# A decoder layer on one core: all transposes on TensorE, v truncated by three engines, and a new order

## The chip, the cores and the metric

The kernel runs on one NeuronCore of a Trainium2 chip. That core has TensorE (PE, matrix products into PSUM), VectorE (DVE), ScalarE (ACT), GpSimd (POOL) and SyncE (SP, which issues the DMAs here). The metric is the device time in microseconds, as the median of several runs. A profile is one further execution, recorded instruction by instruction. Its span runs from the first to the last instruction.

## The reference

One decoder layer, in pre-norm form, on x of 16 x 128 x 256 in float32 with a context of 16 x 128 x 128:

```
x = x + attn(layernorm(x))             # A: fixed-point self attention, 16 heads of 64
x = x + xattn(layernorm(x), ctx)       # B: cross attention to ctx, 16 heads of 64
x = x + ffn(layernorm(x))              # C: two LoRA experts on one shared FFN, 256 -> 1024 -> 256
```

Attention A rounds nearly everything toward zero to a grid of 1/4096:

```
make_fxp(x) = trunc(clip(x, -c, c) * 4096) / 4096
q, k, v = make_fxp(split(x @ w_qkv.T))
dots = make_fxp((q @ k.T) / 8);  attn = make_fxp(softmax(dots))
out = make_fxp(attn @ v);        out = make_fxp(out @ w_proj.T + b_proj)
```

B is a plain softmax attention with an output projection. C adds `top_k_values[k] * relu(x @ (wi + lora_k).T) @ wo.T` over two experts.

## The kernel before

The 16 sequences are worked on as 8 blocks of two (BLK = 2, so 256 tokens, blk 0 to 7). A and B split the 16 heads into two halves of 8 (hf). For each block the program lists its operations in this way: prep A, attn_A for both halves, out_proj A, prep B, ctx_prep, attn_B for both halves, out_proj B, prep C, ffn.

Each operation is recorded first (`Recorder.op`) with its engine, an estimated cost, and the tiles it reads and writes. A list written out by hand, `ORDER` (lines 39 to 119), then gives the order in which the 2,019 recorded operations are emitted. Each engine runs its own operations strictly in that order, and SP issues its DMAs in that order as well. So a wait at the head of one engine's queue holds up everything that stands behind it on that engine. The estimated costs served to make the list; they have no effect on the chip. Several blocks are under way at once: while one block is in attention A, others are in B or C.

Tiles are given slots. In SBUF there are the classes L, M, S and T. In PSUM there are three "big" slots of 4,096 bytes per partition and two "sml" slots of 2,048 bytes. A tile that finds no free slot waits until the last reader of the former owner is done.

To keep float32 accuracy with float16 matrix products, a value is split into hi (float16) and lo (the rest, float16), and a product takes three passes: hi*hi, hi*lo, lo*hi (`PASSES`). So most matmuls are float16 ones of 128x256 (lines 489, 607, 761, 799) or 128x512 (line 499). Scores (line 540) and the product with v of B (line 679) are smaller and run two at a time on halves of the array. The product with v of A (line 583) is float32, and each of those matmuls is two passes in the records.

The parts that the change touches:

- `prep` (lines 424 to 462) normalizes x to xh (float32, tokens on partitions) and needs it transposed as hi and lo, xTh and xTl. For three preps (A of blocks 0 and 1, C of block 7; `BY_PE`) PE transposes xh into a sml PSUM tile pt, ACT copies the hi part out (line 451) and DVE subtracts for the lo part (line 452). For the other 21, ACT makes hi (line 455), DVE makes lo (line 456), and SP issues a DMA transpose of each (lines 457 and 458).
- `attn_A` makes q, k and v as integers on the grid. ACT computes a positive and a negative part in two passes, p and n (lines 507 and 508), and DVE subtracts them; for v that is line 553. After softmax, POOL multiplies by the reciprocal sums and rounds down to int16, one instruction for each of 8 heads (a_A, line 571). SP transposes the tile by DMA (line 574), POOL casts it to float32 (aTf_A, line 576), and PE multiplies with v (line 583).
- `attn_B` has POOL multiply the exponentials by the reciprocal sums (line 660), POOL make the hi part ah (line 661) and DVE the lo part al (line 662). SP transposes both by DMA (line 669), and PE multiplies with v (line 679).
- Another helper, `trunc1` (line 510), truncates in one pass of ACT (line 513) and one of DVE (line 514). Before, it serves only the output of A's attention.

Of the kernel before, what the change touches and what calls it, by code (L numbers as in the profile page):

```python
# [8 lines left out]
F32 = mybir.dt.float32  # L9
F16 = mybir.dt.float16  # L10
# [24 lines left out]
BY_PE = (("A", 0), ("A", 1), ("C", 7))  # L35
NORM_B = "PP"
# [3 lines left out]
1 29 84 85 2 20 323 86 87 324 3 14 5 0 22 325 4 326 17 88 11 327 89 6 8 15 31 90 18 91 12 7 30 42 328 92 94 93 9 19  # L40
98 99 39 16 13 23 802 100 101 10 95 149 150 142 143 102 103 40 152 151 96 104 97 54 33 126 145 144 26 562 447 128
110 153 329 127 105 111 112 106 146 41 563 147 154 129 32 148 108 113 337 330 45 155 130 338 107 131 114 564 132 109
133 43 448 44 134 331 115 381 1042 116 565 382 803 340 339 117 566 449 118 384 388 567 383 385 386 389 56 333 341
332 390 334 177 387 391 392 342 135 156 208 568 178 569 335 119 161 393 1043 804 179 157 120 621 163 162 180 394 336
164 622 628 181 182 159 158 46 623 121 624 136 183 416 160 184 165 55 185 57 137 47 1282 417 629 625 166 626 418 395
396 186 24 122 627 25 343 635 138 209 631 636 167 419 123 398 397 630 51 187 638 168 400 188 577 169 59 637 139 632
805 420 344 633 345 402 401 189 140 578 584 421 27 210 585 170 1044 347 580 579 403 171 124 634 58 190 365 346 349
586 587 172 570 366 191 173 367 28 571 192 35 36 399 581 219 351 174 422 350 404 368 175 220 141 125 640 176 423 424
34 352 405 406 369 639 370 641 193 353 407 425 642 194 643 48 354 573 221 355 454 196 371 222 455 356 195 197 198
656 37 408 456 1283 426 427 199 409 657 658 253 806 200 38 201 410 457 202 52 203 807 659 572 687 205 53 254 204 372  # L50
206 215 216 255 660 574 411 373 257 256 258 217 661 428 374 218 662 249 348 259 250 644 211 429 212 645 1045 688 251
357 252 663 808 49 60 375 261 646 260 809 927 213 376 1046 262 412 647 377 358 868 413 214 582 430 664 378 263 869
359 274 275 861 50 862 575 871 870 264 223 872 360 648 414 265 379 224 276 266 588 863 817 864 277 361 865 362 225
818 363 380 875 415 364 873 819 665 583 431 876 1048 236 278 576 666 878 237 279 877 267 226 866 432 649 820 867 238
268 874 589 879 605 227 433 896 21 591 590 667 606 821 810 239 434 607 668 1522 898 811 228 269 270 592 229 1762 897
650 669 435 593 230 651 812 813 1047 822 492 880 232 231 608 271 436 1763 240 899 824 882 609 652 881 493 241 594
825 242 1284 1049 437 438 272 653 243 207 494 439 1064 440 61 595 670 826 1065 814 596 233 827 1057 495 458 459 441
1058 597 244 273 900 245 610 1066 815 1067 883 1050 598 442 611 1051 1523 816 460 823 280 443 1068 246 234 612 1060
1059 461 884 235 901 1052 1053 671 829 445 845 599 247 600 885 613 847 444 846 654 828 488 282 831 489 902 830 490
601 496 497 281 450 614 886 498 451 1054 615 248 283 1285 903 491 500 602 1055 63 1286 1061 499 616 452 501 284 655  # L60
1108 904 453 1109 1101 617 618 1287 285 1102 502 513 1110 1111 1524 1056 603 619 832 620 887 64 604 446 905 503 888
833 462 906 848 1104 889 672 286 62 673 504 1112 1525 1103 514 1113 1289 1526 1115 1062 65 463 834 515 1063 849 1116
1288 835 505 464 1105 506 674 507 287 1118 1106 1069 836 1117 516 1107 1527 1167 1071 465 675 850 851 475 837 890
509 1529 476 288 1297 517 1070 477 1085 838 928 508 1114 1086 891 478 289 676 1087 290 466 1072 892 907 518 1120 66
908 1298 1119 893 1348 519 1121 839 1349 1300 909 467 1088 1122 840 1299 1528 510 521 1089 1351 1350 1136 852 68 468
929 469 1123 1341 677 1342 479 520 678 1290 1291 1647 511 1137 81 1138 480 471 841 1355 1764 1356 470 1352 1090 1073
894 842 481 1293 853 843 512 1091 1292 522 1344 1343 1139 472 1092 482 523 82 1301 1544 1357 1302 1358 69 1545 483
484 524 473 1546 854 83 679 70 1530 1303 1124 1547 1294 1295 680 1531 1093 1296 525 1304 1074 474 1533 1305 1353
1309 1532 855 1075 71 1345 1325 689 856 1306 844 1307 485 1327 1094 1326 486 1346 1537 1140 1311 910 72 857 1076
1538 1347 1125 487 78 1141 1354 972 1142 1328 291 1077 911 973 526 1534 292 1143 1535 1310 974 1078 895 1407 527 976  # L70
1540 858 1308 1539 1144 977 293 1329 859 975 860 1588 79 1589 1079 528 1145 1126 73 978 1095 1330 681 1360 979 1127
1541 1312 1096 1331 1536 1591 682 74 294 1590 1097 912 1542 1313 67 694 1543 686 1361 695 683 1098 75 1128 1362 1765
696 295 1080 1332 1565 1314 80 1549 685 697 684 913 76 1566 698 1081 1359 699 1146 1550 1567 690 1551 915 1315 1129
1363 691 77 1568 1581 1592 700 1593 1364 1316 692 701 914 1582 693 1130 1376 1317 1082 1318 1569 702 1147 1570 1365
1584 703 1583 1377 1148 1131 1149 1333 529 1319 1378 1132 530 1133 728 704 1595 1379 1366 1596 1585 916 1134 705
1150 531 1594 1598 1552 729 1597 1135 1151 1099 1766 1571 532 730 1083 1320 715 1100 732 1380 1084 733 1548 1367
1767 731 1553 1368 1152 1334 1768 533 736 716 1586 706 1321 1572 535 734 1587 737 738 735 1573 739 1769 917 1381
1153 1554 1322 1555 1600 717 1616 297 534 1770 1335 1154 1556 1771 296 1382 1601 1602 740 1618 1155 1617 1336 938
918 939 1773 1772 1574 298 741 1369 940 1156 1383 1603 1157 707 1337 718 1557 1777 1778 919 941 934 1558 299 1370
1338 719 536 742 1780 935 1575 1599 1779 1371 936 753 300 1158 1339 920 1576 754 301 921 1577 922 302 720 937 743  # L80
923 1559 1372 1373 1168 924 309 1384 310 708 1619 925 1578 303 755 721 1374 304 1560 1561 1774 1385 537 722 968 1775
305 1386 969 1340 1562 311 312 540 756 306 724 1387 538 1323 1324 1620 723 710 970 1781 744 709 971 541 1388 1389
711 539 930 1604 1782 1390 1776 1783 931 313 542 314 543 712 725 932 544 757 1391 1789 726 745 1805 933 1605 545
1791 1784 1806 1606 1807 1790 1375 1607 727 758 1785 980 993 759 1621 1787 1786 994 1159 1808 713 746 1392 981 1160
995 548 996 747 1393 714 307 982 1608 549 942 1161 550 1162 955 315 1622 1609 1394 308 997 1623 316 1395 318 1164
1169 956 551 1610 1163 546 317 547 1396 1165 1397 1624 943 957 319 552 1887 748 958 944 760 1212 1208 749 1213 553
1209 1214 1611 983 321 762 554 750 1579 1216 1210 751 1217 1612 959 1625 1215 1809 960 1211 1792 752 1821 1822 1626
1828 761 1218 1823 1810 984 945 1580 1613 555 1793 1829 998 1398 763 1219 1824 961 764 1825 765 1627 1628 1830 946
1408 1629 1220 1399 1400 1826 1233 1221 985 1234 1831 986 766 1630 1827 1832 1174 767 962 1401 963 947 1833 1175
1614 1222 768 1170 1648 1171 1563 988 556 1235 1834 987 964 1788 1176 1172 948 1177 1173 1402 769 1840 1856 1223 965  # L90
1409 1835 1842 1841 1811 1836 1403 1236 966 1404 989 1857 1166 949 1858 1837 1414 1838 1224 1405 926 1415 1631 558
1182 770 1794 1225 1615 1843 771 1859 1237 951 990 1410 1564 1812 967 1411 950 991 999 1416 1860 992 557 1226 1412
952 1183 1417 1413 1238 1000 1184 560 1195 1406 1185 1196 1239 1844 953 1227 1422 1001 1197 1423 1178 1179 1632 1198
1424 1845 1240 1199 1633 1813 1186 1180 1002 1846 1418 1187 1229 1795 1861 954 1634 1200 772 1181 1649 1419 1242
1435 1003 1635 1796 1241 1448 1228 1436 1243 1004 1005 1420 322 1814 1230 1636 1637 1201 1244 1425 1797 1421 1815
1231 1232 1449 1437 1456 1457 1202 1006 1188 1203 1245 1847 1798 1816 1007 1452 1458 1204 1190 1848 1799 1438 1453
1862 1638 1459 1450 1189 1451 1191 1008 1658 1639 1817 1454 1863 1659 1818 1640 1800 1192 1692 1839 1849 1660 1801
# [19 lines left out]
1037 2003 1521 1992 1986 1760 1761 2008 2010 1040 2004 1041 2012 2007 2005 2006 2009 2011 2013 2014 2015 2017 2016  # L117
2018
"""
WPOOL = ()  # L120
SPLIT_C = (7,)
WARM = 16

# [22 lines left out]
class Recorder:  # L146
    def __init__(self):
        self.ops = []
# [738 lines left out]
```

## Time and profile before

| | |
|---|---|
| runs (three) | 540.81, 542.34, 542.90 us; median 542.34 us |
| profiled execution, whole | 543.11 us |
| its span | 541.3 us, TensorE clock granted 1.000 |
| busy: PE, DVE, ACT, POOL | 514.0, 491.7, 457.9, 337.5 us |
| DMA transposes issued by SP | 138 (aT_A 32, aTh_B 32, aTl_B 32, xTh and xTl 21 each), 2.4 to 3.2 us from issue to landing at the median |

How to read it. A line of a profile's group view names the line of the kernel, the engine, the operation, what it writes and reads, the shape, the count, the busy time in us and the mean length of one instruction in ns. After the second bar stands the idle time of the engine just before them and what ended it. The slices divide the span into 40 equal parts, with a digit for the busy tenths in each. The chain in order of time gives start, length in us, and what ran. The timeline gives start and length in us, the engine, the line, and with x8 the number of instructions taken together. In the view of waits, the numbers are us in total, times, and the longest.

PE's lengths overlap: the records draw a matmul from its start to a modelled end, and the next one starts before that end. For PE the distance between starts is therefore of more use than the length.

### The profile page before, as it was taken

To read this page: it belongs to the slowest core of one execution; us is meant where nothing else is said; L and a number is where in the kernel's file an instruction comes from. 1 tells how busy PE (TensorE), PEld (TensorE's weight loads), DVE (VectorE), ACT (ScalarE), POOL (GpSimd) and SP (SyncE) were. 2 spreads that over 40 slices of the span, in tenths; PEclk is the share of its full clock that TensorE was granted. 3 is DMA by queue.
4 is the path that set the end of the run, shared out by engine and by line. 5 is a ranking of instruction groups with operands and counts; after the bars stand their busy time and mean duration, and the time that the engine had idled before them with its cause. 6 is when DMAs were issued, how large, how long until landed. Compare 5 with 4: busy or idle time off the path is not lost. (4 is left out here: it accounts for less than half of the span.)

```text
span 541.3 us, 15415 instructions
## 1 busy us (share of the span) xinstructions
PE 514.0 (95%) x6144; PEld 417.8 (77%) x6144; DVE 491.7 (91%) x818; ACT 457.9 (85%) x1014; POOL 337.5 (62%) x413
## 2 busy tenths in 40 slices
PE   7989997998989999999999999999999999999997
PEld 6777575877678876877777788877878788887886
DVE  5999899999999999999999988999989998986663
ACT  5999999999999999998998997879676998846331
POOL 1057436965667778646586797578967276847440
PEclk9999999999999999999999999999999999999999
DMA  8812504334452474423336126346935722691011
GB/s 283 295 41 58 142 16 107 70 60 81 75 73 51 98 148 78 99 69 41 62 76 99 23 43 106 61 79 103 150 59 105 127 51 53 116 155 22 11 40 59
DMA packets 137453, 47.17 MB, mean 87 GB/s; under 512 B 125988, under 2 KB 134438, under 8 KB 137382
## 3 DMA queue, kind: packets, MB, share of 16 engines
q1 hardware_dynamic: 137382, 46.20, 42.2%
q8 instruction: 48, 0.79, 0.6%
q14 instruction: 23, 0.19, 0.1%
HBM read 13.41 MB, written 2.10 MB: 29 GB/s over the span
## 5 line engine op out<-in xcount | busy, mean ns | idle before, releaser
L571 POOL TENSOR_SCALAR a_A<-E_A,rc_A 128x128 int16<-128x128 f32 x256 | 123.3, 503 | 49.6 <-DVE rc_A L566 27.5
L645 ACT ACTIVATE E_B<-s_B,mx_B 128x128 f32<-128x128 f32 x256 | 91.1, 419 | 6.7 <-DVE mx_B L641 3.8
L660 POOL TENSOR_TENSOR E_B<-E_B,rc_B 128x1024 f32<-128x1024 f32 x32 | 65.9, 2063 | 36.2 <-DVE rc_B L648 31.8
L645 ACT ACTIVATION_READ_ACCUMULATOR E_B<-s_B,mx_B 128x1 f32 x256 | 64.8, 259 | 0.0
L576 POOL TENSOR_SCALAR aTf_A<-aT_A 128x1024 f32<-128x1024 int16 x32 | 37.9, 1185 | 31.3 <-DMA aT_A<-a_A 18.1
L489 PEld LDWEIGHTS <-wh_A 128*128 128x128 f16 x512 | 49.2, 98 | 10.4 <-issue 2.7
L661 POOL TENSOR_SCALAR ah_B<-E_B 128x1024 f16<-128x1024 f32 x32 | 43.0, 1349 | 11.4 <-DVE al_B L662 5.7
L662 DVE TENSOR_TENSOR al_B<-E_B,ah_B 128x1024 f16<-128x1024 f32 x32 | 43.5, 1365 | 0.9 <-POOL ah_B L661 0.9
L641 DVE TENSOR_REDUCE mx_B<-s_B 128x8 f32<-128x1024 f32 x32 | 38.6, 1210 | 3.7 <-PE s_B L540 3.7
L564 DVE TENSOR_REDUCE sm_A<-E_A 128x8 f32<-128x1024 f32 x32 | 38.4, 1205 | 2.2 <-ACT E_A L562 2.2
L583 PE MATMUL av_A<-aTf_A,v_A 128*64 128x128 f32 x512 | 34.5, 278 | 4.2 <-POOL aTf_A L576 2.8
L508 ACT ACTIVATE n_sA<-s_A 128x1024 int16<-128x1024 f32 x32 | 36.6, 1183 | 2.1 <-PE s_A L540 2.1
L562 ACT ACTIVATE E_A<-p_sA 128x1024 f32<-128x1024 int16 x32 | 37.0, 1178 | 0.4 <-DVE r L779 0.4
L507 ACT ACTIVATE p_sA<-s_A 128x1024 int16<-128x1024 f32 x32 | 37.2, 1181 | 0.0
L761 PE MATMUL u_C<-xTl_C,wh_Ci 128*128 128x256 f16 x128 | 34.9, 273 | 1.2 <-DMA xTl_C<-xlo_C 1.2
L489 PE MATMUL gk_A<-xTh_A,wh_A 128*128 128x256 f16 x128 | 35.0, 273 | 1.0 <-ACT p_gA L507 0.8
L489 PE MATMUL gq_B<-xTh_B,wh_Bq 128*128 128x256 f16 x128 | 34.9, 273 | 0.9 <-DVE kl_B L625 0.8
L489 PE MATMUL gq_B<-xTl_B,wh_Bq 128*128 128x256 f16 x128 | 34.9, 272 | 0.7 <-DMA xTl_B<-xlo_B 0.7
L489 PE MATMUL gq_A<-xTl_A,wh_A 128*128 128x256 f16 x128 | 34.9, 272 | 0.5 <-DVE xTl_A L452 0.5
L761 PE MATMUL u_C<-xTh_C,wh_Ci 128*128 128x256 f16 x128 | 34.9, 273 | 0.3 <-DVE kl_B L625 0.3
L489 PE MATMUL gq_A<-xTh_A,wh_A 128*128 128x256 f16 x128 | 34.9, 273 | 0.2 <-DVE kl_B L625 0.2
L607 PE MATMUL pj_B<-wh_Bo,oh_B 128*128 128x256 f16 x128 | 34.9, 273 | 0.0
(213 smaller groups left out, 2004.4 us busy)
## 6 DMA issues: line engine op xcount, KB each, us to landing
st_A<-in_wqkvT_dram SPq DMA_DIRECT2D x6, 512.0 KB, 7.4
X<-in_x_dram SPq DMA_DIRECT2D x8, 256.0 KB, 6.3
out_dram<-xo SPq DMA_DIRECT2D x16, 128.0 KB, 1.7
st_Ap<-in_wprojT_dram SPq DMA_DIRECT2D x2, 512.0 KB, 9.3
cst<-in_ctxT_dram SPq DMA_DIRECT2D x8, 128.0 KB, 2.8
st_Bq<-in_Wq_dram SPq DMA_DIRECT2D x2, 512.0 KB, 4.3
st_Bo<-in_Wo_dram SPq DMA_DIRECT2D x2, 512.0 KB, 3.9
st_Ci<-in_wiT_dram SPq DMA_DIRECT2D x2, 512.0 KB, 3.8
```

Of the source, the lines that this page charges most:

```text
L489: PE.matmul(o[:, c, :], wv(w, i)[:, k + k0, c * 128:(c + 1) * 128], cols(acts[j], k), start=(n == 0), stop=(n == 3 * nk - 1))
L507: a_op(ncol, lambda: S.activation(p(), view(ps()), AF.Relu, bias=-LAM, scale=scale), [ps], [p], name="p")
L562: a_op(1024, lambda p=p, e=e: S.activation(flat(e()), p(), AF.Exp, bias=0.0, scale=1.0 / 4096.0), [p], [e], name="exp")
L564: v_op(1024, lambda e=e, sm=sm: V.tensor_reduce(sm(), e(), axis=AX.X, op=ALU.add), [e], [sm], name="sum")
L571: G.tensor_scalar(a()[:, h * N:(h + 1) * N], e()[:, h, :], r()[:, h:h + 1], -LAM, ALU.mult, ALU.add)
L576: g_op(1.02, lambda aT=aT, af=af: G.tensor_scalar(af(), aT(), 2.0 ** -12, 0.0, ALU.mult, ALU.add), [aT], [af], name="cast")
L641: v_op(1024, lambda ps=ps, mx=mx: V.tensor_reduce(mx(), ps(), axis=AX.X, op=ALU.min), [ps], [mx], name="max")
L645: S.activation(e()[:, h, :], ps()[:, h, :], AF.Exp, bias=mx()[:, h:h + 1], scale=-1.0, accum_out=sm()[:, h:h + 1])
L660: g_op(1.87, lambda e=e, r=r: G.tensor_tensor(e(), e(), r().unsqueeze(2).to_broadcast([128, HH, N]), ALU.mult), [r], [e], name="norm")
L661: g_op(1.02, lambda e=e, ah=ah: G.tensor_scalar(ah(), flat(e()), 1.0, 0.0, ALU.mult, ALU.add), [e], [ah], name="ahi")
L662: v_op(1024, lambda e=e, ah=ah, al=al: V.tensor_tensor(al(), flat(e()), ah(), ALU.subtract), [e, ah], [al], lock=True, name="alo")
L761: PE.matmul(ps()[:, c, :], wv(w, i)[:, k, c * 128:(c + 1) * 128], cols(xt[j], k), start=(n == 0), stop=(n == 6))
```

## The change

All transposes move to PE, and there is no DMA transpose left.

- prep: all 24 go by PE, so 21 more with four float32 transposes each.
- attn_A: the rounding adds 1024, so that the int16 numbers, read as float16 bits, are ordinary float16 numbers. PE transposes the bits (8 for a tile of 8 heads) into a sml PSUM tile tp_A with a float16 identity, and ACT casts the result to float32 and takes 1024/4096 = 0.25 off again. POOL's cast is gone.
- attn_A, v: `trunc1` takes the place of `trunc`. ACT makes p in one pass, DVE takes the minimum with the other rounding in one pass out of PSUM, and POOL clips and casts to float32 in one pass.
- attn_B: PE transposes the normalized float32 tile in two halves of four heads into sml tiles tp_B. From each half ACT makes the hi part and DVE the lo part out of PSUM. POOL's pass for ah is gone.
- Weights of A's q, k and v are scaled by 4096 on loading instead of by 256, so that the products come out on the integer grid.
- `ORDER` is a new list of 2,062 operations. Estimated costs in the recorder are changed as well. New options (S32_A, S32_B, HH_A) are empty, and CAST_A is "AA", so the branches they would open are not built.

```diff
-BY_PE = (("A", 0), ("A", 1), ("C", 7))
-NORM_B = "PP"
 ORDER = """
...
 """
+S32_A = ()
+S32_B = ()
+HH_A = ()
+CAST_A = "AA"
...
+    ident16 = const.tile([128, 128], F16, name="ident16")
+    S.copy(ident16, ident)
...
-            load_weight(f"A{t}{hf}", kc(wqkvT[:, c0:c0 + 512]), 512)
+            load_weight(f"A{t}{hf}", kc(wqkvT[:, c0:c0 + 512]), 512, ws=4096.0)
...
-        if (key, blk) in BY_PE:
...
-        else:
-            xi, xl = tl("xhi_" + key, "S", [128, BLK * D], F16), tl("xlo_" + key, "S", [128, BLK * D], F16)
-            a_op(512, lambda: S.copy(xi(), fx()), [xh], [xi], name="xhi")
-            v_op(512, lambda: V.tensor_tensor(xl(), fx(), xi(), ALU.subtract), [xh, xi], [xl], lock=True, name="xlo")
-            d_op(230, lambda: SP.dma_start_transpose(th().rearrange("p b c n -> p (b c) n"), xi()), [xi], [th], name="T")
-            d_op(230, lambda: SP.dma_start_transpose(tlo().rearrange("p b c n -> p (b c) n"), xl()), [xl], [tlo], name="T")
+        ps = tl("pt_" + key, "sml", [128, BLK, 2, N], F32)
+
+        def tr():
+            for b in range(BLK):
+                for c in range(2):
+                    PE.transpose(ps()[:, b, c, :], xh()[:, b, c * 128:(c + 1) * 128], ident)
+        p_op(0.44, tr, [xh], [ps], name="tr")
+        a_op(512, lambda: S.copy(th(), ps()), [ps], [th], name="th")
+        v_op(512, lambda: V.tensor_tensor(tlo(), ps(), th(), ALU.subtract), [ps, th], [tlo], name="tl")
...
-        pv, nv = tl("p_gA", "M", [128, 1024], I16), tl("n_gA", "M", [128, 1024], I16)
-        trunc(v_ps, pv, nv, 1024, 4096.0 / WS)
-        v_op(1024, lambda: V.tensor_tensor(flat(v()), pv(), nv(), ALU.subtract), [pv, nv], [v], lock=True, name="v")
+
+        trunc1(v_ps, 1024, "gA", lambda p: g_op(1.12, lambda: G.tensor_scalar(flat(v()), p(), -32767.0, None, ALU.max), [p], [v], name="v"))
...
-            aT = tl("aT_A", "M", [128, HH, N], I16)
-            d_op(460, lambda a=a, aT=aT: SP.dma_start_transpose(aT(), a()), [a], [aT], name="T")
+
+            tp = tl("tp_A", "sml", [128, HH, N], I16)
+
+            def tr(a=a, tp=tp):
+                for h in range(HH):
+                    PE.transpose(tp()[:, h, :].bitcast(F16), a()[:, h * N:(h + 1) * N].bitcast(F16), ident16)
+            p_op(8 * TR16, tr, [a], [tp], name="trA")
             af = tl("aTf_A", "L", [128, HH, N], F32)
-            g_op(1.02, lambda aT=aT, af=af: G.tensor_scalar(af(), aT(), 2.0 ** -12, 0.0, ALU.mult, ALU.add), [aT], [af], name="cast")
+            if CAST_A[b] == "A":
+                a_op(1024, lambda tp=tp, af=af: S.activation(flat(af()), flat(tp()), AF.Identity, bias=-0.25, scale=2.0 ** -12), [tp], [af], name="cast")
...
-                g_op(1.02, lambda e=e, ah=ah: G.tensor_scalar(ah(), flat(e()), 1.0, 0.0, ALU.mult, ALU.add), [e], [ah], name="ahi")
-                v_op(1024, lambda e=e, ah=ah, al=al: V.tensor_tensor(al(), flat(e()), ah(), ALU.subtract), [e, ah], [al], lock=True, name="alo")
...
-            aT = []
-            for s_, a in (("h", ah), ("l", al)):
-                t = tl(f"aT{s_}_B", "M", [128, HH, N], F16)
-                d_op(460, lambda t=t, a=a: SP.dma_start_transpose(t(), a()), [a], [t], name="T")
-                aT.append(t)
+            aT = [tl(f"aT{s_}_B", "M", [128, HH, N], F16) for s_ in "hl"]
+            for i in range(2):
+                tp = tl("tp_B", "sml", [128, HH // 2, N], F32)
+                hs = slice(i * HH // 2, (i + 1) * HH // 2)
+
+                def tr(e=e, tp=tp, i=i):
+                    for h in range(HH // 2):
+                        PE.transpose(tp()[:, h, :], e()[:, i * HH // 2 + h, :], ident)
+                p_op(4 * 0.11, tr, [e], [tp], name="trB")
+                a_op(512, lambda tp=tp, hs=hs, aT=aT: S.copy(flat(aT[0]()[:, hs, :]), flat(tp())), [tp], [aT[0]], name="ahi")
+                v_op(512, lambda tp=tp, hs=hs, aT=aT: V.tensor_tensor(flat(aT[1]()[:, hs, :]), flat(tp()), flat(aT[0]()[:, hs, :]), ALU.subtract), [tp, aT[0]], [aT[1]], name="alo")
```

## The prediction

> **What bounds the kernel now.** I read the page first: shares of the engines, then the slices.
>
> ```profile
> span 541.3 us, 15415 instructions
> PE 514.0 (95%) x6144; PEld 417.8 (77%) x6144; DVE 491.7 (91%) x818; ACT 457.9 (85%) x1014; POOL 337.5 (62%) x413
> ...
> PE   7989997998989999999999999999999999999997
> ...
> DVE  5999899999999999999999988999989998986663
> ACT  5999999999999999998998997879676998846331
> ```
>
> PE is at 9 in nearly every slice, to the end; DVE and ACT fall off in the last fifth. But PE's busy time is drawn with modelled ends (one 128x256 matmul "lasts" 0.27 us), so 95% alone doesn't say that PE can't do more. The spacing of starts does. It comes from the chain that ended last, in order of time, and from PE's own timeline:
>
> ```profile
> 495.64 2.62 PE pj_B L607 x24
> ...
> 509.62 0.44 PE pt_C L449 x4
> ...
> 538.01 0.03 issue
> ```
> ```profile
> 200.31 0.38 PE L499 MATMUL gv_A<-wh_A,xTh_A 128*128 128x512 f16 x1
> ...
> 202.47 0.38 PE L499 MATMUL gv_A<-wh_A,xTl_A 128*128 128x512 f16 x1
> ...
> 203.65 0.25 PE L679 MATMUL av_B<-aTh_B,vh_B 128*64 128x128 f16 x2 [0.58 <-DMA aTh_B<-ah_B]
> ...
> 204.34 0.22 PE L679 MATMUL av_B<-aTh_B,vh_B 128*64 128x128 f16 x2
> ```
> ```profile
> 273.60 0.39 PE L540 MATMUL s_B<-kh_B,ql_B 64*128 64x128 f16 x8
> 273.82 0.39 PE L540 MATMUL s_B<-kl_B,qh_B 64*128 64x128 f16 x8
> 274.14 1.09 PE L583 MATMUL av_A<-aTf_A,v_A 128*64 128x128 f32 x16
> ```
>
> The reader is to see one price for each kind of matmul. 24 of 256 columns take 2.62 us: 0.109 each. Ten of 512 columns take 2.16: 0.216. 24 of av_B take 0.69. Eight of the scores take 0.22 to 0.24, say 0.23. Sixteen float32 passes of av_A last 1.09 from first start to last end; one lasts 0.27, so they are 0.0545 apart. Four float32 transposes take 0.44: 0.11 each.
>
> With the counts of the groups by line: 2,992 of 256 columns x 0.109 = 326.7; 292 of 512 x 0.216 = 63.1; 1,536 of the scores x 0.0288 = 44.2; 512 passes of av_A x 0.0545 = 27.9; 32 av_B jobs x 0.69 = 22.1; warming 6.4; 12 transposes 1.3. Sum 491.7 us of PE work that no order shortens. PE starts at 1.5 and ends at 538.0. So of the span of 541.3, 491.7 is work, 4.8 lies before and after, and 44.8 is lost in gaps between jobs. PE is the bound, with 8% of slack and no more.
>
> What ends the gaps is in the view of waits on PE:
>
> ```profile
> PE av_A L583 <- POOL aTf_A L576: 2.8, 2, 1.5
> ...
> PE av_B L679 <- DMA aTl_B<-al_B: 2.0, 2, 1.3
> ...
> PE u_C L761 <- DMA xTl_C<-xlo_C: 1.2, 1, 1.2
> ```
>
> All waits for DMA transposes are 2.0 + 1.2 + 0.7 + 0.6 = 4.5 us, those for the cast on POOL 2.8. So what the change removes from PE's path is 7.3 us.
>
> **The change, part by part.** PE's work first, as that sets the end.
>
> 1. *Rows of LayerNorm.* 21 prep calls (6 of A, 8 of B, 7 of C) turn from two DMA transposes into four float32 transposes: 84 x 0.11 = 9.2 us on PE.
>
> 2. *Second attention.* 32 softmax tiles of 8 heads in float32: 256 x 0.11 = 28.2 us on PE.
>
> 3. *First attention.* 256 transposes of 128x128 float16 bits. No row has this form. Per transpose 128 weight columns are loaded and 128 columns streamed. The nearest row is av_B: two float16 matmuls of 64 weight columns and 128 streamed ones start in each 0.055 us, so 128 weight columns and 128 columns of streaming pass in 0.055. That gives 256 x 0.055 = 14.1 us. The Trainium skill ("TensorE: Matmul & The Clock Gate", LDWEIGHTS) puts a load at columns / 1.2 ns, 107 ns for 128; if that paced it, 27.4 us. I take 14.1 and keep 27.4 for the range: the row shows the loads keeping up at 0.055.
>
> A rule of the same page (Part 4: PE-mode transpose) speaks harder against the change: about 275 ns for a 128x128 transpose inside a kernel, and a clock gate that doesn't count transposes as work. The trace has both readings: its transposes *last* 272 to 286 ns, but start 110 apart, at a granted clock of 1.00 throughout. By the rule, 596 transposes cost 164 us and the kernel takes about 700; by the row, 37.4 + 14.1 = 51.5. Throughput is what counts in a queue, so I take the row.
>
> New PE work: 491.7 + 51.5 = 543.2 us. With 4.8 around it, the span is 548.0 before the first gap: already 6.7 above the old span with all its gaps.
>
> 4. *ACT.* Added: 32 casts of tp_A (128x1024, like p_sA, 1.18) = 37.8; 64 copies of tp_B (128x512 out of PSUM; L451 takes 0.57) = 36.5. Removed: 16 passes n_gA of v at 1.17 = 18.7. The copies of prep change source: 21 x (0.57 - 0.63) = -1. ACT goes from 457.9 to 512.5 busy. What hides the 54.6 more is PE's own time: 512.5 is less than 543.2. Where a stretch gives ACT more than PE, the difference is counted with the gaps below; were PE faster, ACT would be the next bound.
>
> 5. *DVE.* al_B: 64 subtractions from PSUM at 0.69 (L452) for 32 at 1.37: +0.7. v: 16 at 1.21 (like vl_B) for 16 at 1.36: -2.4. prep: 21 x 0.69 for 16.7: -2.2. About 488: nothing, well under PE.
>
> 6. *POOL.* Loses the casts of aT_A (37.9) and ah_B (43.0), gains 16 of v (1.18 each, as the cast L576) = 18.9: 276. No effect: it isn't near the bound. The stall that goes is the 2.8 counted above; v is late instead only if POOL's queue holds it behind a norm of 8 x 0.5 us, and av_A, which waits for it, needs v after the scores, softmax and transposes.
>
> 7. *SP.* 138 transposes of about 1.2 us of issue leave its queue, some 170 us; the 16 stores and the loads stay. Nothing on PE waited for those but the 4.5 us above. Landing took 3.2 us at the median; PSUM and two engines take that place.
>
> 8. *Weights times 4096, ident16 (one small copy at the start), costs in the recorder*: no time on PE.
>
> **The gaps.** 44.8 before. I cut each order at every 20 us of PE work and added up, between the cuts, what the other engines have to do, at spacings read as above (a 128x1024 pass takes ACT 0.905 of spacing). Before, ACT or DVE has more than PE in 14 of 25 stretches, 28 us in all; after, in 8 of 27, 20 us in all, nearly all between 60 and 160 us. The other 17 us before are handovers over 438 PE jobs, 0.038 each; 555 jobs give 21. That makes 41; taking off a part of the 7.3 us of waits that go leaves 37. The ends: 15 if the new order hides nearly everything, 65 if the new tiles in PSUM hurt.
>
> Sum: 543.2 + 4.8 + 37 = 585.0 us of span. The profiled execution took 543.11 with a span of 541.3, 1.8 more, and the median of the runs, 542.34, is 0.8 below it: **586 us** for the median, 8% slower.
>
> **The rivals.**
>
> *A tight order.* The new order was laid out with transposes on the engine it plans for, and without landings of 2.4 to 5 us it could hide gaps to 15 us: 543.2 + 4.8 + 15 + 1 = 564. For it: in the last 43 us PE already runs without a gap. Against: ACT is as full relative to PE as before (512 of 543, 458 of 492).
>
> *PSUM.* The two small PSUM slots take 225 tiles instead of 108. The new ones stay at least transposing, copying and subtracting: 64 x 1.70 (0.44 + 0.57 + 0.69) + 32 x 1.62 (0.44 + 1.18) + 21 x 1.70 = 196 us more of slot time. A transpose that finds no slot holds up all of PE behind it, and the slot is freed only by ACT or DVE, whose queues are full. With 0.25 us lost at each of the 117 new jobs, +29: about 615. Or the float16 transposes at 0.107: +13, 599.
>
> *Transposes that don't help.* If neither DMA nor POOL waits were what made the gaps, all 44.8 remain and grow per job to 57: 606.
>
> *Faster than before.* It needs one thing: transposes at half my price (0.055 in float32, as av_A's single passes, 0.0275 in float16), so 25.8 for 51.5, in the place where PE has its gaps. Then 491.7 + 25.8 + 4.8 = 522.3, and below 18 us of gaps it beats 542 (15 give about 538). The row of pt_C at 0.11 speaks against it.
>
> **How the numbers follow.** Main case (gaps 25 to 50, 574 to 599) 0.52; tight order 0.22; PSUM, slow float16 transposes or gaps that stay (599 to 625) 0.21; faster 0.03; no change 0.02. The range that leaves out about a tenth on each side is 556 to 608. Within 0.5% of 542.3 is about what these runs can tell from no change: faster 0.03, same 0.02, slower 0.95.
>
> **What would show it.** Right: PE still near 95% with 51 us more starts; the transposes of a float32 tile 0.11 apart, those of float16 0.055; ACT near 512 and DVE near 488 busy; POOL near 276; waits on PE for ACT copies of tp_A and tp_B where DMA stood. Wrong: PE's transposes spaced at half, or PE gaps far under 37 us or over 60.

## The result, and the profile after

The changed kernel takes 597.3 us (median; 594.8 to 599.4), the kernel before 542.6 beside it: a ratio of 1.101 [1.096, 1.106]. Forecast were 586 and a range of 556 to 608. The direction was right; the time is 11 us above the forecast and inside its range. The profiled execution took 598.16, with a span of 596.3.

The page after, its shares and slices:

```profile
span 596.3 us, 16260 instructions
...
PE 569.6 (96%) x6740; PEld 471.4 (79%) x6740; DVE 484.8 (81%) x850; ACT 507.1 (85%) x1095; POOL 277.6 (47%) x365
...
PE   6999987899888999999999999999999999999997
...
DVE  4799989799988788988978996887898698648554
ACT  4999878998999999999999999987976899957432
...
PEclk8999997999999999999999999999999999999999
...
DMA  8930000000000012100000000000000000000002
```

PE is again at 9 from the second third on. DVE and POOL got slack, ACT is at 9 from slice 10 to 25 (149 to 388 us). DMA is empty but for loads and stores. New is the row of the granted clock (PEclk): it drops at slices 0 and 6, while the profile before shows 1.000 on average.

PE's groups by form (busy, mean length, idle before them) and PE's timeline (start, length, instructions taken together):

```profile
L691 PE MATMUL tp_B<-ident,E_B 128*128 128x128 f32 x256 | 38.1, 276 | 1.6 <-ACT xh_C L448 1.0 <-DVE aTl_B L694 0.4 <-DVE p_oA L514 0.2
...
L597 PE MATMUL tp_A<-ident,a_A 128*128 128x128 f16 x256 | 19.6, 219 | 1.0 <-DVE p_oA L514 0.7 <-POOL a_A L590 0.3
```
```profile
306.94 0.61 PE L597 MATMUL tp_A<-ident,a_A 128*128 128x128 f16 x8
...
317.27 0.60 PE L691 MATMUL tp_B<-ident,E_B 128*128 128x128 f32 x4
```

The new transposes are there, and priced as forecast. Eight float16 ones last 0.61 us together and one lasts 0.219, so they start (0.61 - 0.219) / 7 = 0.056 apart. Four float32 ones: (0.60 - 0.276) / 3 = 0.108. The idle time in front of both groups is 2.6 us in all.

With the prediction's own prices the work is 543.2; 596.3 - 543.2 - 4.8 leaves **48.3 us of gaps, where 37 were forecast and 44.8 had been before**. The same subtraction is used for every kernel below. Waits on PE (us in total, times, longest):

```profile
PE gq_A L489 <- DVE xTl_A L458: 3.4, 1, 3.4
PE s_A L560 <- DVE ql_B L652: 2.5, 2, 1.8
...
PE gk_B L489 <- DVE vl_B L652: 1.4, 1, 1.4
PE s_B L560 <- ACT E_B L679: 1.3, 1, 1.3
PE s_A L560 <- ACT E_B L679: 1.3, 2, 1.0
...
PE av_A L610 <- ACT aTf_A L601: 0.2, 1, 0.2
```

No wait for a DMA transpose is left. The new transposes and what reads them wait little: pt_B 1.1, tp_B 1.6, tp_A 1.0, av_B for aTl_B 0.3, av_A for aTf_A 0.2, together 4.2 us, where DMA and POOL had cost 7.3. (The 3.4 us for xTl_A are block 0, which went by PE before as well and then waited 0.5.) The longest waits are for old operations of DVE and ACT. The view counts idle time only after a matmul's modelled end, so its sum, some 23 us, is less than the 48.3. Where PE idles, the windows tell (length, then busy us and count of PE, PEld, DVE, ACT, POOL; clock; DMA share; GB/s):

```profile
60.00:100.00 40.00, 34.88 (x384) 27.52 (x383) 36.91 (x78) 31.90 (x56) 18.58 (x27) 0.96 0.00 1
100.00:140.00 40.00, 37.01 (x393) 28.55 (x392) 35.75 (x63) 36.91 (x89) 27.29 (x39) 0.95 0.01 2
140.00:200.00 60.00, 52.14 (x727) 41.24 (x726) 54.48 (x96) 58.44 (x111) 33.33 (x59) 1.00 0.01 4
200.00:260.00 60.00, 59.77 (x752) 48.35 (x751) 51.47 (x96) 58.08 (x93) 36.02 (x52) 1.00 0.12 39
```

The kernel before, between 140 and 200 us:

```profile
140.00:200.00 60.00, 57.68 (x764) 48.05 (x759) 59.30 (x98) 58.46 (x129) 42.02 (x55) 1.00 0.46 87
```

Three regimes. From 60 to 140 us no engine is full and the clock is below 1. From 140 to 200 ACT is full (58.4 of 60) and PE isn't (52.1); before, ACT was just as full there, but PE got 57.7 done beside it. From 200 on PE is full. So "PE is the bound" holds for the last two thirds only.

Two places in the timeline show the clock. First the start, DVE's queue and PE's:

```profile
8.09 0.43 DVE L439 BATCH_NORM_STATS2 bn_A<-X 128x6 f32<-128x256 f32 x1 [2.06 <-DMA X<-in_x_dram]
...
9.38 1.23 DVE L297 SCALAR_TENSOR_TENSOR wl_A<-st_A,wh_A 128x1024 f16<-128x1024 f32 x1
11.20 0.16 DVE L444 SCALAR_TENSOR_TENSOR nm_A<-mv_A,rs_A 128x2 f32<-128x2 f32 x1 [0.59 <-POOL rs_A L443]
11.27 0.69 DVE L458 TENSOR_TENSOR xTl_A<-pt_A,xTh_A 128x512 f16<-128x512 f32 x1
```
```profile
12.01 0.37 PE L489 MATMUL gq_A<-xTl_A,wh_A 128*128 128x256 f16 x1 [3.41 <-DVE xTl_A L458]
```

The first xTl_A stands in the list behind the statistics of the next block, whose X is late by 2.06 us, behind a weight's lo part and behind a value from POOL. PE waits 3.4 us, and the granted clock is half until 14.9 us. Later, PE's timeline around 100 us:

```profile
100.12 0.42 PE L489 MATMUL gq_A<-xTl_A,wh_A 128*128 128x256 f16 x1
100.34 0.42 PE L489 MATMUL gq_A<-xTh_A,wl_A 128*128 128x256 f16 x1
...
103.81 0.27 PE L489 MATMUL gq_A<-xTh_A,wh_A 128*128 128x256 f16 x1
103.92 0.27 PE L489 MATMUL gq_A<-xTl_A,wh_A 128*128 128x256 f16 x1
```

The same matmul starts 0.21 to 0.22 apart, and from 103.8 us on 0.11 apart. Half clock is granted at 11.5 to 14.9 and 96.8 to 103.6 us, 10.2 us, which fits the mean of 0.991; PE loses at most 10.2 / 2 = 5.1 us by it. The second stretch follows gaps of PE (1.78 and 0.95 us among them) between 85 and 98 us. Before, the mean clock of the profiled execution was 1.000; other executions of that kernel had 0.996 to 1.000.

Last, v's pass on POOL, by the page:

```profile
L572 POOL TENSOR_SCALAR v_A<-p_gA 128x1024 f32<-128x1024 int16 x16 | 46.3, 2898 | 8.9 <-DVE p_gA L514 8.5
```

The prediction took 1.18 us for it, as for a cast of the same shape. It takes 2.90.

### The profile page after: what moved, and what is told of

Read it like the earlier page. It is cut to its first block, busy times and chain, and to the rows that moved or that the text cites. A ratio compares the mean times of both kernels' runs of the same rounds, so it can differ in the third digit from the quotient of the medians.

```text
span 596.3 us, 16260 instructions
## 1 busy us (share of the span) xinstructions
PE 569.6 (96%) x6740; PEld 471.4 (79%) x6740; DVE 484.8 (81%) x850; ACT 507.1 (85%) x1095; POOL 277.6 (47%) x365
## 4 chain that ended last, share of the span: by engine, by line
PE 70%; ACT 14%; DVE 10%; POOL 2%; issue 2%; DMA 1%; SPq 0%; ACTq 0%; DVEq 0%; POOLq 0%
PE u_C L785 6%; PE pj_B L634 6%; PE dn_C L826 6%; PE pj_A L634 5%; PE gk_A L489 5%; PE gq_A L489 5%; PE gv_A L499 5%; PE gq_B L489 4%; PE tp_B L691 4%; PE av_A L610 4%; PE s_B L560 3%; ACT E_B L679 3%; PE av_B L703 3%; PE gk_B L489 2%; PE gv_B L499 2%; ACT p_sA L507 2%
## 5 line engine op out<-in xcount | busy, mean ns | idle before, releaser
L590 POOL TENSOR_SCALAR a_A<-E_A,rc_A 128x128 int16<-128x128 f32 x256 | 109.2, 446 | 76.9 <-DVE rc_A L585 56.0
L683 POOL TENSOR_TENSOR E_B<-E_B,rc_B 128x1024 f32<-128x1024 f32 x32 | 61.5, 1925 | 97.2 <-DVE rc_B L682 94.9
L679 ACT ACTIVATION_READ_ACCUMULATOR E_B<-s_B,mx_B 128x1 f32 x256 | 65.9, 261 | 0.0
L694 DVE TENSOR_TENSOR aTl_B<-tp_B,aTh_B 128x512 f16<-128x512 f32 x64 | 43.2, 682 | 26.4 <-ACT aTh_B L693 25.5
L693 ACT CAST aTh_B<-tp_B 128x512 f16<-128x512 f32 x64 | 39.1, 615 | 16.4 <-PE tp_B L691 16.1
L572 POOL TENSOR_SCALAR v_A<-p_gA 128x1024 f32<-128x1024 int16 x16 | 46.3, 2898 | 8.9 <-DVE p_gA L514 8.5
L691 PE MATMUL tp_B<-ident,E_B 128*128 128x128 f32 x256 | 38.1, 276 | 1.6 <-ACT xh_C L448 1.0
L601 ACT ACTIVATE aTf_A<-tp_A 128x1024 f32<-128x1024 int16 x32 | 34.4, 1101 | 3.1 <-PE tp_A L597 2.2
L489 PE MATMUL gq_A<-xTh_A,wl_A 128*128 128x256 f16 x128 | 36.0, 282 | 0.0
L634 PE MATMUL pj_A<-wl_Ap,oh_A 128*128 128x256 f16 x128 | 34.9, 273 | 0.0
L634 PE MATMUL pj_A<-wh_Ap,ol_A 128*128 128x256 f16 x128 | 34.9, 273 | 0.0
```

Source lines behind the costliest of these rows:

```text
L489: PE.matmul(o[:, c, :], wv(w, i)[:, k + k0, c * 128:(c + 1) * 128], cols(acts[j], k), start=(n == 0), stop=(n == 3 * nk - 1))
L572: trunc1(v_ps, 1024, "gA", lambda p: g_op(1.12, lambda: G.tensor_scalar(flat(v()), p(), -32767.0, None, ALU.max), [p], [v], name="v"))
L590: G.tensor_scalar(a()[:, h * N:(h + 1) * N], e()[:, h, :], r()[:, h:h + 1], 1024.0 - LAM, ALU.mult, ALU.add)
L634: PE.matmul(ps()[:, b, :], o[hf][b][j]()[:, c, :], wv(f"{key}{'p' if key == 'A' else 'o'}{hf}", i)[:, c, :], start=(key == "B" and n == 1) ...
L679: S.activation(e()[:, h, :], ps()[:, h, :], AF.Exp, bias=mx()[:, h:h + 1], scale=-1.0, accum_out=sm()[:, h:h + 1])
L683: g_op(1.87, lambda e=e, r=r: G.tensor_tensor(e(), e(), r().unsqueeze(2).to_broadcast([128, HH, N]), ALU.mult), [r], [e], name="norm")
```

## The experiments

Theory: PE's transposes cost their spacing, 51.5 us, and the order hides a part in old gaps. Rivals: the removed waits paid and something else costs; the round trips through PSUM and ACT cost; the new order costs.

**1. PE's work alone, in the old order.** 936 float16 transposes (52.4 us at 0.056) ahead of the scores, into the PSUM tile that the scores then overwrite. Nothing reads them.

```diff
+        extra = 21 + (len(count_s) % 4 == 0) if ps.name == "s_B" else 8
         def fn():
+            for d in range(extra):
+                src = (q, k)[d // 8 % 2][0]
+                PE.transpose(ps()[:, d % 8, 0:64].bitcast(F16), src()[:, (d % 8) * 128:(d % 8 + 1) * 128], ident16)
```

> The kernel before in its own order, its DMA transposes kept, with 936 more float16 transposes on PE in front of the scores (8 in each tile of A, 21 or 22 in each of B, of the hi parts of q and k into the PSUM tile that the scores then overwrite; nobody reads them). At 0.056 each that is 52.4 us of PE work, what the change adds, and no work for ACT, DVE, POOL or PSUM slots. PE as the bound: 542 + 52 less up to 12 that fall into gaps, 582 to 596. Rival, that the change loses its time by ACT's load, PSUM slots or the order: PE work alone fills the 45 us of gaps, under 560.

Measured: 583.1 us, 1.074 [1.070, 1.077]. The page:

```profile
span 582.6 us, 17289 instructions
...
PE 568.7 (98%) x7080; PEld 471.7 (81%) x7080; DVE 492.7 (85%) x818; ACT 461.7 (79%) x1015; POOL 328.2 (56%) x413
```

52.4 us of PE work cost 40.8, 0.78 for one, with ACT, DVE and POOL nearly as before. Gaps are 582.6 - 491.7 - 52.4 - 4.8 = 33.7: 11 us went into old gaps. So as much PE work as the change adds, with nothing else, is enough for 41 of its 55 us. That is in the old order, with the work in front of the scores and not where the change has it. The remaining 14 are 597.3 - 583.1.

**2. The change's order with DMA transposes.** All transposes by DMA again, each new operation put where PE's stood; v by three engines.

```diff
+BY_PE = (("A", 0), ("A", 1), ("C", 7))
-                    PE.transpose(tp()[:, h, :].bitcast(F16), a()[:, h * N:(h + 1) * N].bitcast(F16), ident16)
+            d_op(460, lambda a=a, aT=aT: SP.dma_start_transpose(aT(), a()), [a], [aT], name="T")
...
```

> The changed kernel in its new order with all three groups of transposes given back to DMA (and the passes of POOL, ACT and DVE that go with them); v by three engines and the order stay. PE as the bound and an order that is neither better nor worse: 597 - 51 = 546, between 538 and 556. If the new order itself cost time: over 560. If it hides more than the old one: under 538.

Measured: 808.7 us, 1.490 [1.485, 1.495]. Far outside 538 to 556; the expectation's "over 560" would blame the new order itself. A DVE group:

```profile
L685 DVE TENSOR_TENSOR al_B<-E_B,ah_B 128x1024 f16<-128x1024 f32 x32 | 49.3, 1540 | 106.4 <-POOL ah_B L684 96.1 <-POOL aTf_A L602 10.3
```

DVE stands 96 us at the head of its queue for POOL's hi parts, as the list, laid out for the short way, puts too little work between them. The mean granted clock is 0.854, so the clock was at half for some 2 x 0.146 x 806.6 = 236 us, which costs PE up to half of that (an estimate): the waits came with a slower clock. This says what operations at ill-fitting places of a list cost. It says nothing of PE's price, nor of what the new order is worth to its own operations.

**3. v by three engines alone, in the old order.** Only `trunc1` for v and the weights' factor; POOL's pass as times 1 plus 0, without the clip.

```diff
-        trunc(v_ps, pv, nv, 1024, 4096.0 / WS)
-        v_op(1024, lambda: V.tensor_tensor(flat(v()), pv(), nv(), ALU.subtract), [pv, nv], [v], lock=True, name="v")
+        trunc1(v_ps, 1024, "gA", lambda p: g_op(1.12, lambda: G.tensor_scalar(flat(v()), p(), 1.0, 0.0, ALU.mult, ALU.add), [p], [v], name="v"))
```

> The kernel before with v alone changed: one pass each of ACT, DVE and POOL (POOL's pass written as times 1 plus 0, without the clip at -32767), weights of A times 4096. ACT loses 14.5 us of spacing, POOL gains 18. PE as the bound everywhere: 542 within 3. Rival: in the first 140 us ACT is full and sets the pace, so 5 to 10 us are won: 532 to 537.

Measured: 677.0 us, 1.246 [1.242, 1.252], a miss by over 100 us. POOL's group:

```profile
L549 POOL TENSOR_SCALAR v_A<-p_gA 128x1024 f32<-128x1024 int16 x16 | 20.3, 1270 | 88.9 <-DVE p_gA L512 66.1 <-DVE sm_A L561 9.4 <-DVE rc_A L562 6.2
```

The pass stands in POOL's list where the old one of DVE stood, so POOL waits at its head for DVE, 66 us, and norms and casts behind it wait too. Here as well the clock fell, to 0.917 in the mean. What v is worth, this can't say.

**4. Another form of v's pass, all else as in the change.**

```diff
-G.tensor_scalar(flat(v()), p(), -32767.0, None, ALU.max)
+G.tensor_scalar(flat(v()), p(), 1.0, 0.0, ALU.mult, ALU.add)
```

> The changed kernel with POOL's pass for v written as times 1 plus 0 in place of the maximum with -32767 (no clip). In the profile the pass took 2.77 us where the old cast of the same shape took 1.19. I expect 1.2 us for it. PE as the bound with POOL 47% busy: 597 within 4. Rival: v late or norms behind it on POOL make gaps on PE: 585 to 592.

Measured: 592.1 us, 1.091 [1.088, 1.094], about 5 less than the change, whose interval begins at 1.096. That is between the two forecasts (593 to 601 with PE as the bound, 585 to 592 for the rival).

```profile
L572 POOL TENSOR_SCALAR v_A<-p_gA 128x1024 f32<-128x1024 int16 x16 | 18.3, 1150 | 10.4 <-DVE p_gA L514 10.2
```

The pass over one shape and type takes 1.15 or 2.90 us, by its form. Gaps are 590.6 - 543.2 - 4.8 = 42.6. Not all of the 5.7 us between the two profiles is the pass: xTl_A came earlier at the start here (PE waited 1.9 for it, not 3.4), and there was no half clock after it. Both kernels have the same list, so the n-th PE instruction of one can be set beside that of the other: of the 5.7 us, 2.5 are there by 20 us, before the first pass on v starts (29 us). At most 3.2 are left for the pass. Executions with the same mean clock agree: at 0.994 they took 594.8 and 591.8 us, at 0.997 596.5 and 592.8.

**5 to 10. One search of orders for six sets of operations.** To compare groups of transposes on fair ground, each set got an order from one planner, made with the durations measured here: before's own operations (re_before); all by DMA with the new v (re_v3); all on PE (re_full); on PE only the rows of LayerNorm (re_P), the first attention (re_A) or the second (re_B). All but re_before have v's pass in the form of experiment 4. The edits are those of the change, group by group, and a new list:

```diff
-ORDER = """..."""
+ORDER = """..."""   # searched
```

> The operations of the kernel before, untouched, in an order that was searched anew (the old order as the start, single operations moved as long as gaps closed by the measured spacings). The control for the runs that share this search. PE work stays 491.7, so no less than 497; if the 45 us of gaps are a matter of order: 530 to 540; if they are not: 541 to 546.

> All transposes by DMA, v by three engines (POOL's pass as times 1 plus 0, no clip), order searched anew in the same way. Differs from the control by v alone. ACT loses 14.5 us of spacing of 444: if ACT's fullness in the first 140 us makes gaps on PE, 3 to 8 under the control; if PE's work is all that counts, within 3 of it. The earlier run of this change in a shifted old order, 677, would then be the order's doing.

> All transposes by PE, v by three engines (POOL's pass without the clip), order searched anew in the same way. PE as the bound: 51 above the run with all transposes by DMA in the same kind of order, give or take 8, so 575 to 592. Rival, that the changed kernel's own order is what cost the time: under 560.

> As the run with all transposes by DMA in a searched order, but the 21 transposes of LayerNorm's rows on PE. 84 float32 transposes of 0.109 are 9.2 us of PE work, against two landings of 2.4 us and a queue on SP: 5 to 12 above that run if PE is the bound; within 3 or below, if the shorter way from x to the first matmuls is worth as much.

> As the run with all transposes by DMA in a searched order, but the first attention's on PE: 256 float16 transposes of 0.056, 14.3 us of PE work, and ACT gets 32 casts (29 us of spacing) that POOL had. PE as the bound: 12 to 20 above that run. If a full ACT is what costs: over 22. If the DMA way was itself a cost: under 10.

> As the run with all transposes by DMA in a searched order, but the second attention's on PE: 256 float32 transposes of 0.109, 28 us of PE work, ACT gets 64 copies (31 us of spacing), POOL loses 32 passes, and two small PSUM slots take 64 more tiles. PE as the bound: 25 to 33 above that run. PSUM slots: over 38.

| kernel | us | ratio |
|---|---|---|
| re_before | 605.7 | 1.116 [1.110, 1.122] |
| re_v3 | 568.8 | 1.047 [1.042, 1.052] |
| re_full | 605.5 | 1.115 [1.110, 1.120] |
| re_P | 594.0 | 1.094 [1.089, 1.099] |
| re_A | 593.9 | 1.091 [1.087, 1.095] |
| re_B | 588.5 | 1.080 [1.076, 1.084] |

The control fails: the operations of before, only in another order, take 63 us more, where 530 to 546 was expected. The largest of its waits on PE:

```profile
PE av_A L581 <- POOL aTf_A L574: 15.0, 5, 6.9
```

Its mean clock is 0.960, some 48 us at half, so up to 24 of the 63 us are the clock (an estimate). So these orders are no fair ground. Against re_v3, all on PE costs 37 us, and the three groups 25, 25 and 20, which sum to 70: the noise of an order is tens of us. They agree with the theory in sign only (none on PE is fastest, all on PE slowest of the five). What one group costs stays open.

**11. Transposes at half price, in the change's own order.** On experiment 4: the 352 float32 transposes (96 of pt, 256 of tp_B) become float16 products that read the upper halves of the values. The lower halves are left out, so the result isn't the reference's; the work of the other engines stays.

```diff
-PE.transpose(tp()[:, h, :], e()[:, i * HH // 2 + h, :], ident)
+PE.matmul(tp()[:, h, :], e()[:, i * HH // 2 + h, :].bitcast(F16).rearrange("p (n w) -> p n w", w=2)[:, :, 1], ident16, start=True, stop=True)
```

> The changed kernel in its own order with POOL's pass for v without the clip (592 before), and with its 352 float32 transposes replaced by float16 products with the identity that read the upper halves of the same tiles and fill the same PSUM tiles: the result is not the reference's, but ACT, DVE, POOL, PSUM slots, waits and order stay. At 0.055 for 0.109 that takes 19 us off PE. PE as the bound: 573 to 577. As in the run that only added PE work, four fifths of it: about 577. If the round trip over PSUM and ACT is what costs: over 585. If the products are paced at 0.107 by their weight loads: no change.

Measured: 587.6 us, 1.081 [1.076, 1.086]. That is 1.091 to 1.081 for 352 x (0.109 - 0.056) = 18.7 us less work on PE: some 5.6 us, not the 15 to 19 of a kernel that PE alone binds. Gaps grow from 42.6 to 585.1 - (543.2 - 18.7) - 4.8 = 55.8. By the expectation's own sign (over 585) the round trip through PSUM and ACT would be what costs. The trace shows the price, and two places where time went:

```profile
312.26 0.39 PE L691 MATMUL tp_B<-ident,E_B 128*128 128x128 f16 x4
```
```profile
417.76 3.98 DVE L441 TENSOR_SCALAR rs_B<-mv_B 128x2 f32<-128x2 f32 x1
...
424.99 0.32 PE L703 MATMUL av_B<-aTh_B,vh_B 128*64 128x128 f16 x2 [2.18 <-DVE X L646]
```

Again the n-th PE instruction can be set beside that of experiment 4, to see where the 18.7 us were won and where not (one execution of each, 5.5 us apart):

| stretch (us, experiment 4) | PE work taken away | time won |
|---|---|---|
| 0 to 20 | 0.4 | -1.9 |
| 20 to 320 | 6.4 | 2.6 |
| 320 to 420 | 4.7 | 3.5 |
| 420 to 430 | 0.6 | -3.2 |
| 430 to the end | 6.6 | 4.5 |

At the start PE waits 2.5 us for xTl_A, 0.5 more than in experiment 4, and the clock is at half for 3.4 us behind it, as it was not there. At 420 us a small addition on DVE, which takes 0.2 to 1.1 us elsewhere in this kernel, takes 3.98 and ends with POOL's passes; PE waits 2.2 us for what stands behind it, and another 3.4 us at half clock follow. At both places PE waits for DVE, not for ACT: the first time for xTl_A, the second, as it seems, for a small PSUM slot that DVE has still to read (av_B doesn't read X). These two places take 6.1 of the 13.1 us that were not won. Elsewhere 10.6 of 17.7 us were won, 0.6 of each us. The window from 140 to 200 us:

```profile
140.00:200.00 60.00, 52.42 (x718) 42.06 (x714) 52.50 (x96) 59.73 (x115) 32.85 (x63) 1.00 0.01 4
```

ACT is busy 59.7 of 60 and PE 52.4. But less than 0.9 us of PE work was taken away in this stretch, and about half of it was won, so a full ACT there can't hold back much of the 13.1.

**12. Half of the casts from ACT to DVE.** Also on experiment 4.

```diff
-CAST_A = "AA"
+CAST_A = "AV"
```

> The changed kernel in its own order with POOL's pass for v without the clip (592 before), and with the casts of every second tile of the first attention on DVE in place of ACT: 16 passes, 14.5 us of spacing less on ACT and some 18 more on DVE. If ACT, at 58 of 60 us busy from 140 to 320, makes part of the gaps: 585 to 589. If only PE's work counts: 592 within 3. If the casts hold up DVE's queue in an order not made for them: 595 to 605.

Measured: 598.3 us, 1.100 [1.097, 1.104], by the ratios 5 more than without, as forecast for casts that hold up DVE's queue. Waits on PE:

```profile
PE tp_A L597 <- DVE aTf_A L603: 1.8, 2, 1.3
PE av_A L610 <- DVE aTf_A L603: 1.7, 4, 0.5
```

The cast waits in DVE's queue, and PE behind it for the slot of tp_A and for av_A. An emptier ACT didn't pay with the work at an ill-fitting place of another queue. The same window as above:

```profile
140.00:200.00 60.00, 52.39 (x727) 41.84 (x723) 54.62 (x97) 56.69 (x111) 31.58 (x62) 1.00 0.02 4
```

ACT has 3 us less to do here than in experiments 4 and 11 (56.7 instead of 59.7), DVE 2 to 3 us more, and PE does no more than there (52.4; 52.8 in experiment 4). So that ACT holds PE in this stretch is not shown; no run took work from ACT without giving it to another busy engine.

No kernel tried beats the one before.

## Why the prediction was right or wrong

**PE's price: right.** 0.109 and 0.056 by spacing, against 0.11 and 0.055 forecast; summed over the groups at their median spacings, PE's work rose by 50.2 us for 51.5. The Trainium skill's 275 ns for one transpose ("TensorE: Matmul & The Clock Gate", Part 4) is here the length of one (276), not what the next one waits, and no load of 107 ns paced the float16 ones at 0.056. That the clock gate doesn't count transposes is neither confirmed nor refuted: the clock was 1.00 in all windows from 140 us on, but there the transposes stand among many more other matmuls (68 of 752 between 200 and 260 us).

**PE carries the slowdown: right for the larger part.** Experiment 1 gets 41 of the 55 us with nothing but PE work, in the old order. In the new order PE isn't the only bound: taking PE work away (experiment 11) won 0.6 of it outside two places, and 0.3 with them.

**Waits that go: right, and small.** DMA's 4.5 and POOL's 2.8 are gone, 4.2 came in their place.

**The sums of the others: right but for one term, v on POOL.** ACT 507.1 (512.5 forecast), DVE 484.8 (488). POOL's 277.6 for 276 is chance: v took 46.3 instead of 18.9, and three other terms came out lower: the int16 norms 109.2 instead of the 123.3 of before, B's norms 61.5 instead of 65.9, and passes of C (hh and hl) 31.3 instead of 35.8.

**The gaps: the term that was mis-sized, 48.3 for 37.** The step said that handovers stay at 0.038 a job, that full ACT or DVE add 20, and that something comes off for waits that go. What it left out is seen in three places:

- v's pass at 2.90 us. With the other form, and an earlier start in that execution, the gaps are 42.6: 5.7 of the 11.3 us are gone, at most 3.2 of them by the pass.
- The start and the half clock. PE waits 3.4 us for xTl_A (0.5 before), and 10.2 us at half clock cost up to 5.1. The step took the granted clock of before, 1.000, to stay. These overlap with the line above; the start differs between the profiles.
- The stretch from 60 to 160 us of PE work, where the step put nearly all of its 20 us. Counted from the trace as distances between starts beyond each kind's median, 27 of some 52 us of gaps lie there: the right place, with more in it. "512.5 is less than 543.2, so PE's time hides it" is right as a sum; by stretches ACT is full from 140 to 200 us while PE idles. That ACT is the cause is not shown (experiments 11 and 12), and what makes the excess stays open.

How the last 14 us (583 to 597) divide between ACT's load, the round trips, the order, v and the start, no run tells cleanly: 592 to 597 is v and the start, 583 to 592 is the rest together.

**The rivals.** *Tight order* (564): out. *PSUM* (29 us lost at the new jobs, 615): the waits at new jobs are 4.2, and at all jobs that write a small PSUM slot 5.4 (the warm-up left out), where it was 7.8 before; out. Its variant with slow float16 transposes (599) came near in time by chance, as they are 0.056 apart and not 0.107. *Transposes that don't help* (606, all gaps stay and grow to 57): 48.3, about half way between the 37 of the forecast and this. *Faster* needed spacings of 0.055 and 0.0275, which aren't there; and experiment 11, which gave the float32 ones nearly that price but left the float16 ones at 0.056, still took 588.

## What to carry to other kernels

Price a TensorE operation by the distance between starts, not by its length, and ask of every stretch, not of the whole span, whether PE is full: work taken from it won 0.4 of itself between 20 and 320 us of experiment 11, and 0.8 between 320 and 420. An operation that moves to another engine needs a new place in that engine's queue: in an order written out as a list, operations put at the places of others cost 135 us over the kernel before and 211 over the changed one (experiments 3 and 2), and another order of the same work 63. Look at the granted clock of such runs too: it was 0.917, 0.854 and 0.960.

## What the runs showed of the hardware

- On POOL, a tensor_scalar from int16 to float32 over 128x1024 with one operation, max against a constant, took 2.90 us; with two, times 1 plus 0, 1.15.
- TensorE's granted clock fell to half for 3.4 and 6.8 us in the changed kernel, after waits of PE of 3.4 us, and of 1.78 and 0.95; the matmuls of 256 columns then start 0.21 apart instead of 0.11. In experiment 4 PE waited 1.95 us at the same place of the start, and the matmuls went on at 0.11; at 92 to 95 us it waited 1.97 and 0.96, and 3.4 us at half followed. In experiment 1 it fell for 3.4 us at 11.3 us, with no single wait over 1.5 us ahead of it. So the length of one wait doesn't decide it here; what does isn't settled by these runs.
- Within the spans of all these profiles, stretches at half clock last 3.4 us or a multiple of it (3.4, 6.8, 10.2, 13.7, 17.1, 20.5).
- A DVE addition over 128x2 took 3.98 us once, in experiment 11, and at most 1.13 otherwise in that kernel. It ended at 421.74 us, as a run of POOL passes did (421.71).
- One microsecond of PE work cost 0.78 added to the old order. Taken from the new one it won 0.30, or 0.6 outside the two places of experiment 11.
